# Transpositions of two subchunks at once in the first layer of a four-layer kernel: alternating halves of the array, shared operand tiles

## The chip, the core and the metric

The kernel runs on one core of a Trainium2 chip. Its engines are TensorE (PE in the profile, its weight loads PEld), VectorE (DVE), ScalarE (ACT), GpSimd (POOL) and SyncE (SP), which here only issues DMAs. Matrix products go to PSUM[...]; VectorE and ScalarE carry them from there to SBUF. The metric is the device time of one execution in microseconds (us). All data are 32-bit floats.

## What is computed

Four layers in a row on 8 images of 56 x 56 positions with 192 channels. Only the first is touched. Cut to what matters:

```python
def first_layer(x):                         # x: [8, 56, 56, 192], group-normalised before
    p, q, v = silu(x @ p_w.T + p_b), silu(x @ q_w.T + q_b), silu(x @ v_w.T + v_b)   # 576 channels each
    a1 = rpe_mlp(rpe_input, t1) * decay     # 112 coefficients for each channel
    a2 = rpe_mlp(rpe_input, t2) * decay
    qv = q * v
    o1 = toeplitz(qv along w, a1)           # for each channel a product with a 56 x 56 Toeplitz matrix
    o2 = toeplitz(qv along h, a2)           # the same along the other axis
    return x + (p * (o1 + o2)) @ o_w.T + o_b
```

For each channel d the kernel must form `qv[d] @ A1[d] + A2[d] @ qv[d]` with 56 x 56 matrices. It does both products with one matrix product over 120 partitions: the left operand holds the transposed `qv[d]` in 56 partitions and a Toeplitz matrix in 56 others, the right operand the other two.

## The kernel before, in words

**Tiling.** The 576 channels are 9 subchunks of 64. Two of them make a chunk: chunks 0 to 3 hold subchunks (0,1), (2,3), (4,5), (6,7); chunk 4 is the tail with subchunk 8 alone. In the code `n` counts subchunks through all images, `b` is the image, `c` the chunk.

**What happens to a chunk.**

1. `project` (L283): q and v of the chunk, in four steps `g` of 2 x 7 rows of the image. A step's products (L294 for 128 of the input channels, L301 for the other 64, which lie in two halves of the partitions) go to two PSUM tiles (one in the tail). ScalarE applies SiLU (L310), and `multiply` (L316) writes q*v into the tile `qv` twice, in both orders of rows and columns: "straight" by VectorE (L319), "across" by GpSimd (L325), in the last step partly by VectorE (also L325).
2. `turn` (L342), for one subchunk: 56 transpositions (L352), one for each row position `i`, each of 64 channels by 120 positions out of `qv`, with a piece of the identity matrix. They go into PSUM in steps of up to 16 (16, 16, 16, 8 make 56), eight positions to a bank. After each step VectorE copies partitions 0 to 55 into the left operand and ScalarE partitions 64 to 119 into the right one (both L359). Subchunks with even number lie in partitions 0 to 63 of `qv`, odd ones in 64 to 127; `turn(n)` and then `turn(n + 1)` each stay in one of these halves.
3. `convolve` (L363), for one subchunk: two steps of 32 products (L376) over 120 partitions; results are copied to the tile `ot` (L396 by VectorE, L394 by ScalarE, L387 in the tail).
4. `post` (L407) after chunks 1 and 3, `post_tail` (L495) after the tail: p (`gate`, L417, L424, SiLU L431), transposing `ot` back (`back`, L442) and multiplying (L451 by VectorE), the output product (`out`, L462, L467) and its addition into `acca` and `accb` (L403, L405 by VectorE). `in_turn` orders them: step g is `back(g - 1)`, `gate(g)`, `out(g - 1)`; nine steps in `post`, four in `post_tail`, where the products are L507, L514, L541 and L553, the transpositions L528 and the multiplication L534.

**Operands.** `pairs` (L257) holds two left and two right operand tiles (`ol`, `or`), used by even and odd subchunks. The Toeplitz halves are loaded by `toeplitz(n)` (L265): from the coefficients (`ed`) in the first image, which also writes ready tables (`tt`); from these tables later. `toeplitz(m + 2)` is issued behind `convolve(m)`, on SP's queue.

**PSUM.** One pool of four tiles of two banks each serves the layer, in turn (`banks`, L159): the fifth request waits until the first tile has been read.

**Order.** TensorE's order is that of the program text. `merge(a, b)` (L595) interleaves two lists of steps over as many rounds as the longer has; of the shorter list it places each step at the end of its share of rounds. The loop at L615 does for each chunk: `merge(fill, turns)`, where `fill` is the `post` of the chunks before, if there is one; then `project` of the next chunk, merged with `beside` (statistics and normalisation of images, L98 to L130, L49 and L576); then the convolutions. In chunk 3 `project` of the tail and the convolutions alternate step by step instead (L643). So the transpositions of chunk 0 lie beside the `post_tail` of the image before, those of chunk 2 beside `post(0)`, those of chunk 4 beside `post(1)`; those of chunks 1 and 3 stand alone. The order on the other engines is a scheduler's.

Of the kernel before, what the change touches and what calls it, by code (L numbers as in the profile page):

```python
# [17 lines left out]
H = 56  # L18
# [38 lines left out]
def image_dma(queue, dram, xa, xb, store=False):  # L57


    parts = []  # L60
    for at in range(0, HW, HQ // 2):
        cols = slice(at, at + HQ // 2)
        parts.append((xa[0:CP, cols], dram[:, 0, cols]))
        parts.append((xa[CP:CA, cols], dram[0 : CA - CP, 1, cols]))
        h, own = at // HQ, slice(at % HQ, at % HQ + HQ // 2)
        parts.append((xb[h * CB : (h + 1) * CB, own], dram[CA - CP :, 1, cols]))
    for s, d in parts:
        if store:
            queue.dma_start(d, s)
        else:  # L70
            queue.dma_start(s, d)


def sub(ap, *dims):

    return bass.AP(ap.tensor, ap.offset, [list(ap.ap[0]), *(list(d) for d in dims)])
# [59 lines left out]
def layer0(cx, xin, xout, w, consts):  # L136
# [6 lines left out]
    tc, nc = cx.tc, cx.nc  # L143
    B = len(xin)
    NS, DS = 9, 64
    NC = 5
    NP = 112
    T2, T1 = slice(0, H), slice(64, 64 + H)
    cx.open(B)
    cx.between = ExitStack()  # L150
    with ExitStack() as es:
        gn = GroupNormSplit(cx, cx.between, w["gmat"])
        cp = es.enter_context(tc.tile_pool(name="l0c", bufs=1))
# [5 lines left out]
        def banks():  # L159
            return cx.tile(psc, [128, 2, 512], "c")  # L160
# [4 lines left out]
        def load_raw(b):  # L165
            xa, xb = cx.tile(np_, [CA, HW], "xa"), cx.tile(np_, [128, HQ], "xb")
            image_dma(nc.sync, xin[b], xa, xb)
            return xa, xb
# [3 lines left out]
        ident = cx.tile(cp, [128, 128], "ident")  # L172
# [10 lines left out]
        with ExitStack() as pes:  # L183
# [11 lines left out]
            n = 1  # L195
# [10 lines left out]
            for t in (1, 2):  # L206
# [13 lines left out]
                for i in range(3):  # L220
                    ps = banks()[0:32, 0, 0:NP]
# [3 lines left out]
                e = cx.tile(pp, [DS, NS, NP], f"e{t}")  # L225
                for s in range(NS):
                    ps = banks()[0:DS, 0, 0:NP]
# [23 lines left out]
        qv = cx.tile(cp, [128, H, 120], "qv")  # L251
# [2 lines left out]


        ND = DS * H
        pairs = [tuple(cx.tile(cp, [120, ND + 8], f"o{k}{i}") for k in "lr") for i in range(2)]  # L257
        for pair in pairs:
            for i, t in enumerate(pair):
                (nc.gpsimd, nc.vector)[i].memset(t, 0.0)  # L260

        def channels(t):
            return t[:, 0:ND].rearrange("p (d i) -> p d i", i=H)
# [52 lines left out]
        def multiply(g, rows, ts):  # L316

            def straight():
                nc.vector.tensor_tensor(  # L319
                    sub(qv[rows, 7 * g :, 64 + H - 1 :], (HH * 120, 2), (120, 7), (-1, H)),  # L320
                    *(t.rearrange("p u (h w) -> p u h w", w=H) for t in ts), ALU.mult,
                )

            def across(eng, u, w0, w1):
                eng.tensor_tensor(  # L325
                    sub(qv[rows, w0:, H - 1 - 7 * g - HH * u :], (120, w1 - w0), (-1, 7)),
                    *(t[:, u].rearrange("p (h w) -> p w h", w=H)[:, w0:w1] for t in ts), ALU.mult,
                )

            if g < 3:  # L330
                straight()
                for u in range(2):
                    across(nc.gpsimd, u, 0, H)
                return

            for i, w in enumerate(((0, HH), (HH, H))):
                across(nc.gpsimd, 0, *w)
                across(nc.vector, 1, *w)
                if i == 0:
                    straight()  # L340

        def turn(n):  # L342

            s = n % NS
            e = s % 2 * DS
            left, right = pairs[n % 2]

            def step(i0, ni):
                ps = banks()[0:120]
                view = lambda k: ps[:, k].rearrange("p (d i) -> p d i", i=8)  # L350
                for i in range(ni):
                    nc.tensor.transpose(  # L352
                        view(i // 8)[:, :, i % 8], qv[e : e + DS, i0 + i, :],
                        ident[e : e + DS, e : e + DS],
                    )
                src = ps[:, 0 : ni // 8].rearrange("p k (d i) -> p d k i", i=8)
                for t, rows, copy in ((left, T2, nc.vector.tensor_copy), (right, T1, nc.scalar.copy)):
                    dst = channels(t)[rows, :, i0 : i0 + ni].rearrange("p d (k i) -> p d k i", i=8)
                    copy(dst, src[rows])  # L359

            return [lambda i0=i0: step(i0, min(16, H - i0)) for i0 in range(0, H, 16)]
# [203 lines left out]
        def normalize(xn):  # L565

            measures, deviate, settle = gn.steps(*xn)

            def measure():
                for f in measures:  # L570
                    f()

            def last():
                rstd, nbias = settle(bank)
                affine(nc.vector, xn[0], xn[0], rstd[:, 0:1], nbias[:, 0:1])
                nc.scalar.activation(  # L576
                    xn[1], xn[1], AF.Identity, bias=nbias[:, 1:2], scale=rstd[:, 1:2]
                )

            return [measure, lambda: deviate(bank), last]  # L580

        def tell(b, xa, xb):

            measures, deviate, settle = gn.steps(xa, xb)

            def last(bank):
                nn = cx.tile(gn.small, [128, 2, 2], "nn")
                for i, v in enumerate(settle(bank)):
                    nc.vector.tensor_copy(nn[:, :, i], v)
                nc.sync.dma_start(cx.norms[b][0:CA], nn[:, 0, :])  # L590
                nc.sync.dma_start(cx.norms[b][CA:], nn[0:CB, 1, :])

            return measures, [deviate, last]

        def merge(a, b):  # L595

            n = max(len(a), len(b))
            for i in range(n):
                for x in (a, b):
                    for f in x[i * len(x) // n : (i + 1) * len(x) // n]:  # L600
                        f()

        def new_acc(b):
            acc = cx.tile(xp, [CA, HW], "acca"), cx.tile(xp, [128, HQ], "accb")
            image_dma(nc.sync, xin[b], *acc)
            return acc

        es.enter_context(tc.manual_schedule(engines={mybir.EngineType.PE}))
        xn, nxt = first, None
        merge(normalize(xn), [])  # L610
        for n in range(2):
            toeplitz(n)
        merge(project(xn, 0), [])
        fill, after, telling = [], None, []
        for b in range(B):  # L615
            more = b + 1 < B
            for c in range(NC):
                n = b * NS + 2 * c
                two = c < NC - 1
                turns = turn(n) + (turn(n + 1) if two else [])  # L620
                merge(fill, turns)
                fill, beside = [], []
                if c == 0:
                    if after is not None:
                        image_dma(nc.sync, xout[b - 1], *after, store=True)
                        beside, telling = tell(b - 1, *after)
                    if more:
                        nxt = load_raw(b + 1)
                if c == 1:
                    acc = new_acc(b)  # L630
                    beside = [lambda f=f: f(bank) for f in telling]
                if c == 2 and more:
                    beside = normalize(nxt)

                if c % 2 == 0:
                    ot = cx.tile(cp, [120, 128, H] if two else [H, H, DS], "ot")
                ahead = project(xn, c + 1) if two else project(nxt, 0) if more else []
                convs = []
                for m in (n, n + 1) if two else (n,):
                    *some, last = convolve(m, ot)  # L640
                    convs += some + [lambda m=m, last=last: (last(), toeplitz(m + 2))]

                if c == NC - 2:  # L643
                    ahead = [f for pair in zip(ahead, convs[0:4]) for f in pair]
                    convs = convs[4:]
                merge(ahead, beside)
                for f in convs:
                    f()
                if c in (1, 3):
                    fill = post(c // 2, xn, ot, acc)  # L650
            fill, after = post_tail(xn, ot, acc), acc
            xn = nxt
# [1386 lines left out]
```

## Time and profile before

| | us |
|---|---|
| median of 3 runs | 4290.92 |
| lowest and highest | 4286.24, 4291.43 |
| the profiled execution | 4297.32 |
| its span, from first to last instruction | 4295.5 |

| engine | busy us | share of the span |
|---|---|---|
| PE | 4052.9 | 94% |
| PEld | 2655.7 | 62% |
| DVE | 2340.9 | 54% |
| ACT | 1781.9 | 41% |
| POOL | 1510.6 | 35% |

The profile is one execution. Its groups of instructions are read as: line, engine, operation, output <- inputs, shapes and count, then busy time in us and the mean of one in ns, then the idle time of the engine just before them and what ended it. Matrix products are pipelined: the mean of one is its latency, and busy time over count tells how often one is finished. "The chain" is the work that ended last, followed back from the end; its pieces are start, length, what. Slices of the span are 40 equal parts, with the busy share in tenths. "Stages" are stretches of the span in which busy time of each engine is summed.

### The profile page before, as it was taken

How to read it: one execution, taken by the hardware profiler on the slowest of the kernel's cores; microseconds unless marked ns; L12 is line 12 of the kernel's file. 1: busy time of each engine (PE TensorE's matmuls, PEld its weight loads, DVE VectorE, ACT ScalarE, POOL GpSimd, SP SyncE). 2: the span in 40 equal slices, each digit the busy share in tenths (PEclk: the TensorE clock that was granted, in tenths of full speed). 3: DMA queues.
4: the chain of work that ended last, by engine and by line, in shares of the span. 5: the costliest groups of instructions: out<-in, count | busy, mean ns of one | idle time of the engine just before them, and what ended most of it. 6: DMA issues, size and time to landing. Idle time of an engine off the chain costs nothing.

```text
span 4295.5 us, 106533 instructions
## 1 busy us (share of the span) xinstructions
PE 4052.9 (94%) x46380; PEld 2655.7 (62%) x46380; DVE 2340.9 (54%) x3429; ACT 1781.9 (41%) x2052; POOL 1510.6 (35%) x1295
## 2 busy tenths in 40 slices
PE   6999999999999999999699999769998999998997
PEld 4666767676676767667366666524444555555997
DVE  4446565554656545554444444366665666664664
ACT  2334434334443333443233344223334555554664
POOL 3223232222322222232133333133334444444776
PEclk9999999999999999999899999889999999999999
DMA  6755242242524224241224344455547676664243
GB/s 137 143 106 144 61 114 62 78 96 61 143 62 111 56 74 109 61 109 59 80 72 109 96 107 105 121 173 171 165 140 180 171 174 156 155 152 114 71 117 93
DMA packets 379607, 484.14 MB, mean 113 GB/s; under 512 B 175780, under 2 KB 324372, under 8 KB 377236
## 3 DMA queue, kind: packets, MB, share of 16 engines
q1 hardware_dynamic: 373636, 466.97, 42.8%
q10 hardware_dynamic: 5504, 10.35, 0.8%
q8 instruction: 365, 5.98, 0.6%
q14 instruction: 102, 0.84, 0.1%
HBM read 321.49 MB, written 155.65 MB: 111 GB/s over the span
## 4 chain that ended last, share of the span: by engine, by line
PE 79%; DVE 6%; issue 5%; SPq 3%; DMA 3%; ACT 2%; POOL 1%; DVEq 0%; ACTq 0%; POOLq 0%
PE c L294 10%; PE c L376 6%; PE v L1371 6%; PE c L301 5%; PE c L462 4%; PE c L417 4%; PE c L924 4%; PE h L1873 4%; PE c L352 4%; PE y L959 3%; PE kv L1431 3%; PE c L442 3%; PE c L424 3%; DVE ol L359 2%; PE c L1583 2%
## 5 line engine op out<-in xcount | busy, mean ns | idle before, releaser
L325 POOL TENSOR_TENSOR qv<-s,s 128x392 f32<-128x392 f32 (+3 forms) x320 | 568.5, 1798 | 1453.5 <-ACT s L310 1453.0
L310 ACT ACTIVATE s<-c,bqv 128x784 f32<-128x784 f32 (+1 forms) x320 | 278.2, 910 | 383.9 <-PE c L301 189.1
L294 PE MATMUL c<-xa,wqv 128*128 128x392 f32 x1152 | 433.2, 518 | 4.3 <-DVE xa L49 2.7
L359 ACT COPY or<-c 56x1024 f32<-56x1024 f32 (+1 forms) x288 | 256.2, 901 | 424.4 <-DVE ol L359 414.5
L319 DVE TENSOR_TENSOR qv<-s,s 128x784 f32<-128x784 f32 (+1 forms) x160 | 205.8, 1287 | 265.0 <-ACT s L310 265.0
L359 DVE COPY ol<-c 56x1024 f32<-56x1024 f32 (+1 forms) x288 | 299.8, 1076 | 39.8 <-PE c L352 38.5
L294 PEld LDWEIGHTS c<-xa,wqv 128*128 128x128 f32 x1152 | 211.1, 194 | 176.8 <-issue 39.3
L376 PEld LDWEIGHTS c<-or,ol 120*64 120x64 f32 x9216 | 275.8, 139 | 39.5 <-issue 29.6
L376 PE MATMUL c<-or,ol 120*64 120x56 f32 x9216 | 284.5, 223 | 11.5 <-DMA ol<-ed 7.7
L352 PEld LDWEIGHTS c<-ident,qv 64*120 64x120 f32 x4032 | 256.1, 138 | 55.1 <-issue 35.6
L352 PE MATMUL c<-ident,qv 64*120 64x64 f32 x4032 | 282.8, 224 | 3.6 <-POOL qv L325 2.5
L1371 PE MATMUL v<-wvb,wa 128*128 128x512 f32 (+1 forms) x400 | 192.1, 612 | 50.5 <-ACT wa L1282 31.3
L301 PE MATMUL c<-xb,wqv 64*128 64x392 f32 x1152 | 232.9, 518 | 0.0
L431 ACT ACTIVATE s<-c,bp 128x448 f32<-128x448 f32 x224 | 129.7, 630 | 248.7 <-PE c L424 248.6
L1904 POOL TENSOR_TENSOR y<-y,s 128x448 f32<-128x448 f32 x168 | 185.0, 1101 | 92.7 <-ACT s L1883 92.7
L1873 PE MATMUL h<-ringv,am 128*64 128x57 f32 (+1 forms) x4400 | 192.7, 235 | 19.6 <-DVE ringv L1860 11.8
L462 PE MATMUL c<-po,wo 128*128 128x448 f32 x448 | 198.1, 564 | 7.0 <-DVE po L451 7.0
L1873 PE MATMUL h<-ringh,am 128*64 128x57 f32 (+1 forms) x4400 | 186.3, 232 | 7.8 <-DVE ringh L1879 7.8
L1382 ACT ACTIVATE vb<-sm 128x1024 f32<-128x1024 f32 (+1 forms) x100 | 103.7, 1038 | 212.2 <-issue 187.2
L417 PE MATMUL c<-xa,wp 128*128 128x224 f32 x896 | 191.1, 356 | 0.0
L405 DVE TENSOR_TENSOR acca<-c,acca 128x392 f32<-128x392 f32 (+1 forms) x120 | 67.3, 587 | 219.2 <-PE c L467 204.8
L1873 PEld LDWEIGHTS h<-ringv,am 128*64 128x64 f32 x4400 | 168.1, 140 | 22.9 <-DVE ringv L1860 12.7
(221 smaller groups left out, 7591.9 us busy)
## 6 DMA issues: line engine op xcount, KB each, us to landing
or<-tt SPq DMA_DIRECT2D x252, 196.0 KB
ol<-tt SPq DMA_DIRECT2D x252, 196.0 KB
vt<-v SPq DMA_DIRECT2D x56, 672.0 KB
v<-vb SPq DMA_DIRECT2D x96, 384.0 KB
x<-x SPq DMA_DIRECT2D x112, 168.0 KB
x<-x SPq DMA_DIRECT2D x112, 112.0 KB
bt<-bs SPq DMA_DIRECT2D x28, 448.0 KB
bs<-bs SPq DMA_DIRECT2D x56, 224.0 KB
```

The lines of the kernel that those rows point to most:

```text
L294: nc.tensor.matmul(ps[:, h, 0:n], wqv[0][:, j, :], xn[0][:, at : at + n], start=True, stop=False,)
L301: nc.tensor.matmul(ps[:, h, 0:n], wqv[1][rows, j, :], xn[1][rows, g * n : (g + 1) * n], start=False, stop=True,)
L310: nc.scalar.activation(t, ps[rows, :, 0:n], AF.Silu, bias=bqv[rows, j : j + 1])
L319: nc.vector.tensor_tensor(sub(qv[rows, 7 * g :, 64 + H - 1 :], (HH * 120, 2), (120, 7), (-1, H)), *(t.rearrange("p u (h w) -> p u h w", w= ...
L325: eng.tensor_tensor(sub(qv[rows, w0:, H - 1 - 7 * g - HH * u :], (120, w1 - w0), (-1, 7)), *(t[:, u].rearrange("p (h w) -> p w h", w=H)[:, ...
L352: nc.tensor.transpose(view(i // 8)[:, :, i % 8], qv[e : e + DS, i0 + i, :], ident[e : e + DS, e : e + DS],)
L359: copy(dst, src[rows])
L376: nc.tensor.matmul(ps[u * 64 : (u + 1) * 64, k, v * H : (v + 1) * H], left[:, d * H : d * H + 64], right[:, d * H : (d + 1) * H], start=Tr ...
L417: nc.tensor.matmul(out(u, h), wp[0][:, 2 * j + u, :], xn[0][:, at : at + n], start=(u == 0), stop=True, skip_group_check=True,)
L462: nc.tensor.matmul(pa, wo[:, 2 * j + u, 0:CA], pos[u], start=(u == 0), stop=(u == 1))
L1371: nc.tensor.matmul(out, x[:, at : at + n], wt, start=(k == 0), stop=(k == 1), skip_group_check=True,)
L1873: nc.tensor.matmul(ps[sides[c], y], am[a][:, m * CB : (m + 1) * CB], old[:, x], start=(n < 2), stop=True, skip_group_check=True,)
```

## The change

- The operand tiles become one left and one right tile (`both`), each with the operands of both subchunks: `[120, 2, 64 * 56 + 8]`. `pairs` are views into them.
- A new `turn_both(n)` takes the place of `turn(n) + turn(n + 1)` in chunks 0 to 3. It has seven steps. In each, for eight row positions, one transposition of the subchunk in partitions 0 to 63 and one of that in 64 to 127 follow each other; each subchunk has its own PSUM bank. One copy by VectorE then takes both subchunks' left parts and one by ScalarE both right parts: `56 x 2 x 64 x 8` elements, 1024 in each partition as before, written in runs of 8 where it was 16.
- The tail keeps `turn(n)`.
- `merge` rounds the other way: each step of the shorter list comes at the start of its share of rounds. This holds for all its calls: transpositions beside `post`, `project` beside statistics and normalisation.

```diff
-        pairs = [tuple(cx.tile(cp, [120, ND + 8], f"o{k}{i}") for k in "lr") for i in range(2)]
-        for pair in pairs:
-            for i, t in enumerate(pair):
-                (nc.gpsimd, nc.vector)[i].memset(t, 0.0)
+        both = [cx.tile(cp, [120, 2, ND + 8], f"o{k}") for k in "lr"]
+        for i, t in enumerate(both):
+            (nc.gpsimd, nc.vector)[i].memset(t, 0.0)
+        pairs = [tuple(t[:, k] for t in both) for k in range(2)]
...
+        def turn_both(n):
+
+            order = (n % 2, 1 - n % 2)
+
+            def step(i0):
+                ps = banks()[0:120]
+                view = ps.rearrange("p k (d i) -> p k d i", i=8)
+                for i in range(8):
+                    for e, k in enumerate(order):
+                        rows = slice(e * DS, (e + 1) * DS)
+                        nc.tensor.transpose(
+                            view[:, k, :, i], qv[rows, i0 + i, :], ident[rows, rows]
+                        )
+                for t, rows, copy in zip(both, (T2, T1), (nc.vector.tensor_copy, nc.scalar.copy)):
+                    dst = t[rows, :, 0:ND].rearrange("p k (d i) -> p k d i", i=H)
+                    copy(dst[:, :, :, i0 : i0 + 8], view[rows])
+
+            return [lambda i0=i0: step(i0) for i0 in range(0, H, 8)]
...
             n = max(len(a), len(b))
             for i in range(n):
                 for x in (a, b):
-                    for f in x[i * len(x) // n : (i + 1) * len(x) // n]:
+                    for f in x[-(-i * len(x) // n) : -(-(i + 1) * len(x) // n)]:
                         f()
...
-                turns = turn(n) + (turn(n + 1) if two else [])
+                turns = turn_both(n) if two else turn(n)
```

## The prediction

> **What bounds the kernel now.** I read the two halves of the page first. The first layer is the part of the span before about 2080 us, eight images at about 251 us each.
>
> ```profile
> PE   6999999999999999999699999769998999998997
> PE 79%; DVE 6%; issue 5%; SPq 3%; DMA 3%; ACT 2%; POOL 1%; DVEq 0%; ACTq 0%; POOLq 0%
> ```
>
> TensorE is at 9 in nearly every slice of the first layer, and 79% of the chain is its own work. So time taken from TensorE there shortens the run, unless something else is close behind it. Next, the costliest groups, for the lines that the change touches:
>
> ```profile
> L359 ACT COPY or<-c 56x1024 f32<-56x1024 f32 (+1 forms) x288 | 256.2, 901 | 424.4 <-DVE ol L359 414.5
> L359 DVE COPY ol<-c 56x1024 f32<-56x1024 f32 (+1 forms) x288 | 299.8, 1076 | 39.8 <-PE c L352 38.5
> L352 PE MATMUL c<-ident,qv 64*120 64x64 f32 x4032 | 282.8, 224 | 3.6 <-POOL qv L325 2.5
> ```
>
> 4032 transpositions keep PE busy for 282.8 us, 70 ns each; their copies keep VectorE busy for 299.8 us. The two are equal. ScalarE's copy of a step always starts after VectorE's (414.5 of its 424.4 us idle): a step is evacuated in series, VectorE then ScalarE. Then I cut one image (the third, and chunk 0 of the fourth) into stages:
>
> ```profile
> 661.00:712.00 51.00, 51.00 (x365) 36.33 (x365) 22.40 (x35) 16.77 (x23) 0.00 (x0) 1.00 0.28 56
> 739.00:746.20 7.20, 7.11 (x111) 6.63 (x110) 6.30 (x7) 5.27 (x6) 0.00 (x0) 1.00 0.88 252
> 833.20:853.30 20.10, 20.01 (x207) 12.45 (x205) 17.57 (x24) 10.26 (x11) 0.21 (x1) 0.92 0.66 182
> ```
>
> The columns are length, then PE, weight loads, DVE, ACT and POOL. Beside `post` (661 to 712) VectorE is busy 44%: TensorE alone bounds. With transpositions alone (739 to 746) and beside the tail's `post` (833 to 853) VectorE is at 87%. The chain says what ends the middle one:
>
> ```profile
> 738.78 1.10 PE c L352 x16
> 739.88 0.02 issue
> 739.90 5.22 DVE ol L359 x5
> 745.12 0.02 issue
> 745.14 1.01 ACT or L359
> 746.15 0.04 issue
> 746.20 1.58 PE c L294 x4
> 747.78 0.86 PE c L301 x4
> 748.64 2.01 PE c L376 x64
> ```
>
> One step of 16 transpositions, five copies on VectorE (four of 1.14 us and one half-size of 0.66), one on ScalarE, and only then `project` gets a PSUM buffer. This stage is bound by the evacuation already.
>
> **How fast alternation can be.** The trace of before has no alternating transposition. It has these:
>
> ```profile
> 601.40 2.83 PE c L294 x8
> 604.23 1.52 PE c L301 x8
> ```
>
> ```profile
> 3292.13 0.81 PE c L1569 x56
> ```
>
> L294 has 128 rows; L301 has 64 and goes from half to half: 354 against 190 ns an instruction of 392 columns. L1569 goes round four 64x64 tiles at 14.5 ns an instruction, weight loads of 64 columns included, 58 ns a tile: about what a lone transposition of 64 columns takes (68), so four tiles hide each other wholly.
>
> [...] The new copies write runs of 8 floats[...] where the old wrote 16. No run here shows the new pattern.
>
> **The change part by part.** Call S the time of 16 transpositions. It is 1.09 us now. With full overlap each half does 8 at 68 ns, offset by half a one: 0.58. If instead the weight loads of the two halves are serial, S is worse: L352's loads of 120 columns last 138 ns, like the plain 64-column loads of L467 (136), where plain 128-column ones last 191 (L417); 64 more plain columns cost 55 ns, so I estimate that a transposition's load occupies some 50 ns, and 16 in series 0.8. With no overlap S stays 1.09. I take 0.58: L1569's 58 ns for four 64-column loads excludes serial loading.
>
> A pair of subchunks has 8 steps (six of 16, two of 8: 6 x 1.09 + 2 x 0.61 = 7.76 us of PE) and gets 7 (7S = 4.06). VectorE's copies go from 6 x 1.14 + 2 x 0.66 = 8.16 us to 7 x 1.14 = 7.98: nothing to gain there. By stage and image:
>
> - *Chunk 2, beside `post`.* PE saves 7.76 - 4.06 = 3.70. At the end `back(6)`, one step and `out(6)` follow each other; `out` waits for VectorE's product, which is behind two additions (1.05), the copy before (1.21) and takes 0.63. Before, the 1.09 us step covered this. Counted from the start of the last step but one, the product is there at 3.1 us and PE at 0.58 + 1.08 + 0.58 = 2.24: 0.85 lost. In mid-stage the 2.48 us of `gate` cover the product as before. Gain 2.85.
> - *Chunk 1, alone.* `project` needs the buffer of the fourth copy, now 4 x 1.14 instead of 5.22, and the first copy comes earlier. But VectorE arrives with the backlog of chunk 0 (18 us of copies, additions and statistics that don't shrink, in a stage 1 us shorter), so the first copy starts about 1.0 us into the stage instead of 1.12. 1.0 + 4.56 + 1.02 + 0.04 = 6.62 against 7.43: gain 0.8.
> - *Chunk 3, alone.* Here `convolve` is interleaved with the tail's `project`, and its first step needs subchunk n complete. Before, n was complete after four copies; now both are complete only after seven. S + 0.02 + 7.98 + 1.02 + 0.04 = 9.64 us to the first L376, against 748.64 - 738.78 = 9.86: gain 0.2. The 2.44 us of `project` lie within this wait. This is where the saving of PE is lost.
> - *Chunk 0, beside the tail's `post`.* VectorE's 17.6 us do not shrink. Following the new order by hand (gate, step, back, gate, out, two steps, back, two steps, out, two steps), `project`'s first buffer is freed by the additions of the last `out`, 19.1 us after the convolutions' end; PE's last step ends there too. It is 20.1 now: gain 1.0, give or take 1.
> - *Chunk 4, still one subchunk.* The steps come one place earlier. The stall before the last `out`, 0.95 us (L462 at 808.69, PE free at 807.73), now has no step in front: back(6) at 1.69, product and latency to 2.55, so 0.86. Gain 0.1. The first step, moved ahead, needs GpSimd's first half of L325; that is done about 1 us before PE gets there.
> - *Normalisation one step earlier* (the new rounding in `merge`). ScalarE's table loads (1.28 us each) and the 1.70 us scaling now come before the last SiLU and delay it by about 1.5 us; the convolutions (7.7 us) hide it and leave some 2 us. Nothing, or 1 us an image if that cover fails.
> - *Waits of the shared tile.* The table loads of SP still wait for the convolution of their own subchunk, and are issued in the same order. No new wait.
>
> Sum: 2.85 + 0.8 + 0.2 + 1.0 + 0.1 = 4.95 us an image; seven images 35. The first has no tail beside chunk 0, and its chunk 3 waits for a table load anyway (14.65 us of DMA in the chain at 235.61); I count 5 for it. Together 40 us: the profiled execution, 4295.5 of span and 4297.3 in all, would become 4257; the median of the runs shown, 4290.9, which is 6.4 below it, 4251.
>
> **The rivals.** A measurement of this kernel can tell about 0.2% (9 us) from no change.
>
> - *Loads partly serial* (S = 0.8): chunk 2 gains 7.76 - 5.60 - 0.63 = 1.5, the others 0.65, 0, 0.85, 0.1: 3.1 an image, 25 us, 4266. For it: L424 alternates too and takes 120 ns where L417 takes 190, less than half off. Against: L1569.
> - *No overlap at all* (S = 1.09), the change not doing what it says: chunk 2 loses 0.2, chunk 3 0.3, the others gain 0.9 together: 0.4 an image, 4288, no change. Against it stands L301.
> - *Slower: the copies' short runs.* If runs of 8 cost VectorE more, all seven copies of chunks 0 and 3 and four of chunk 1 lengthen the path, 18 an image, plus one in chunk 2. L325 on VectorE, with runs of 7 and strided reads, takes 540 ns for 196 elements where a copy of 2 elements (L121) takes 159: 1.9 ns an element against 1.0. At that price a copy costs 0.9 us more: 17 us an image lost, 12 net, 8 x 12 = 97, 4388. It decides from 0.26 us a copy (4.95 / 19). [...]
>
> **How the numbers follow.** Full overlap 0.58, own range 4238 to 4263 (chunk 0's give or take 1 and the first image's 5). Partly serial 0.17. No overlap 0.10. Slower copies, or another wait of that size, 0.11. A gain above 55 us 0.04. Faster by over 0.2%: 0.58 + 0.17 + 0.04 less the edge of the second, 0.78. Within 0.2%: 0.11. Slower: 0.11. The range leaves out the slow rival and the large gain: 4236 to 4290.
>
> **What would show it.** Right: L352 near 36 ns of PE busy each for the paired ones; ol copies still near 1.14 us each in a row; in chunk 3 a wait of L376 for ScalarE's last copy; VectorE's share in the chain up; an image 5 us shorter. Wrong: L352 still at 65 to 70 ns; a copy over 1.3 us; a DMA ahead of L376 in images after the first; GpSimd ahead of L352.

## The result, and the profile after

| | before | after |
|---|---|---|
| median | 4291.18 us (4 runs) | 4258.02 us (4 runs) |
| lowest and highest | 4286.24, 4297.21 | 4253.59, 4265.11 |
| span of the profiled execution | 4295.5 | 4263.3 |

The ratio is 0.9924, with an interval of 0.9905 to 0.9942: 33 us faster. The forecast was 4251, with a range of 4236 to 4290. Of the four executions after, the profiled one was the slowest (4265.11).

The page of the kernel after, first the chain of waits by engine, then the groups of the touched lines, in the columns named above (L352 keeps its number, VectorE's and ScalarE's copies are now L357, the convolution is L395):

```profile
PE 73%; DVE 7%; issue 7%; DMA 4%; SPq 3%; POOL 3%; ACT 2%; DVEq 0%; POOLq 0%; ACTq 0%
...
L357 DVE COPY ol<-c 56x1024 f32<-56x1024 f32 x224 | 261.4, 1208 | 63.4 <-PE c L352 63.4
...
L352 PE MATMUL c<-ident,qv 64*120 64x64 f32 x3584 | 144.3, 227 | 44.2 <-ACT or L357 38.3
```

A transposition in pairs occupies PE for 144.3 / 3584 = 40 ns, where it was 70. The copies are as long as before: 1208 ns for 1024 elements. New is the last column of L352: PE now stands before its transpositions for 44.2 us, nearly all of it until ScalarE's copy. TensorE's share of the chain fell from 79% to 73%. TensorE now waits more for the engines that empty PSUM.

A table by stage shows where the 33 us came from. It is worked out from the start times of TensorE's instructions in the traces; means over images 1 to 7 (counted from 0, so that the third image is image 2), in us. A stage runs from the start of the last convolution before it to the first product of what follows, and the convolutions of chunk 1 from their first to their last product:

| stage | before | after | late_norm | old_rounding | no_alternation | steps_only | fill_chunk1 |
|---|---|---|---|---|---|---|---|
| chunk 0, beside the tail's `post` | 20.07 | 19.80 | 19.43 | 20.67 | 20.14 | 21.01 | 19.42 |
| chunk 1, alone, then `project` of chunk 2 | 27.89 | 26.21 | 26.49 | 26.16 | 26.68 | 26.56 | 24.90 |
| convolutions of chunk 1 | 7.49 | 8.54 | 7.47 | 7.55 | 8.69 | 7.51 | 7.47 |
| chunk 2, beside `post(0)` | 51.27 | 49.21 | 48.24 | 48.39 | 50.34 | 49.86 | 48.24 |
| chunk 3, to its first convolution | 10.02 | 10.11 | 10.13 | 10.22 | 10.80 | 10.31 | 10.23 |
| chunk 4, beside `post(1)` | 48.31 | 48.15 | 48.15 | 48.30 | 48.15 | 48.31 | 48.15 |
| start of the layer's last 128 convolution products, at | 2075.8 | 2045.6 | 2028.7 | 2036.8 | 2066.2 | 2057.4 | 2017.5 |

The last five columns are experiments 1, 4, 3, 4 and 6 below. The last row stands for the end of the layer; what follows it, with the last `post_tail` and the three untouched layers, took 2207 to 2220 us in these seven. Each column is one execution, and the profiled one is not always a middling one: 7 us above the median in the kernel after, 6 us below it in late_norm, 15 us below it in old_rounding. So a difference between last rows carries these offsets, and a stage is the safer evidence where its seven images agree.

**Chunk 2, beside `post`.** The end of this stage in the third image, in the chain of the kernel after (start, length, what):

```profile
693.00 0.61 PE c L352 x16
693.62 1.10 PE c L461 x8
...
695.14 0.61 DVE po L470
695.75 0.04 issue
695.80 1.77 PE c L481 x4
```

A step of 16 takes 0.61 us. Behind `back(6)` (L461) TensorE waits 1.08 us for VectorE's product (L470), which stands behind a copy. Five of seven images take 48.24 to 48.32 here, 3.0 less than before; image 6 took 54.32, see the first experiment.

**Chunk 3.** The same view, fourth image:

```profile
975.04 0.64 PE c L352 x16
...
975.70 8.02 DVE ol L357 x7
...
983.74 1.01 ACT or L357
...
984.79 2.15 PE c L395 x64
```

Seven copies of VectorE in a row, 1.14 us each, one of ScalarE, and then the convolution: 975.04 to 984.79 is 9.75 us. What TensorE saved lies within these 8 us.

**Chunk 1.** The same view, third image:

```profile
618.79 1.01 ACT or L357
619.80 0.04 issue
619.85 1.11 PE c L352 x16
620.96 0.02 issue
620.98 3.92 PE c L294 x8
```

A step of 0.61 us takes 1.11 and L294 takes 3.92 in place of 2.83. The windows of the two stretches (length, busy PE, weight loads, DVE, ACT, POOL, then the granted clock, the DMA engines' busy share and GB/s) say why:

```profile
613.00:619.80 6.80, 5.02 (x152) 4.54 (x148) 5.44 (x5) 3.93 (x4) 0.00 (x0) 0.99 0.86 213
619.80:625.20 5.40, 5.33 (x26) 3.15 (x28) 3.48 (x4) 4.03 (x4) 0.00 (x0) 0.70 0.96 231
```

The granted clock averages 0.70 behind a stretch in which TensorE was busy for 5.02 of 6.80 us.

**The convolutions of chunk 1** are the only stage that got clearly longer. Chain of the kernel after, fourth image:

```profile
890.57 7.60 PE c L395 x254
898.17 1.67 issue
899.84 0.32 PE c L395 x2
```

TensorE stops for 1.67 us, two records from the end of a step of 64, with no engine named. Five other images have stops of 0.3 to 0.9 us elsewhere, within a step too (after 153 records in the third); image 6 has none here. A wait for a PSUM tile would stand at the start of a step. The page has a queue of the kind "instruction":

```profile
q8 instruction: 365, 5.98, 0.6%
```

These are 365 blocks of 16 KB. The queue is taken for TensorE's: in the packet records of both traces, of before and after, one block starts for each 256.0 of TensorE's instructions (2 x 46380 = 92760 in the page, 93467 and 93474 with those of its sequencers), and none lies more than 0.93 of a block off that line. Counted by the instructions of VectorE, ScalarE, GpSimd or SyncE, some lie 18 to 35 blocks off. Beside the stop the packet records have a block that arrives at 898.29 (897.40 and 0.89 us under way), and TensorE goes on at 899.84, 1.55 us later. In this layer TensorE takes instructions fastest in a convolution stage, 512 in 7.5 us. What is different in this stage is what `merge` puts beside the `project` ahead of it. In chunk 1 that is the end of the statistics of the image before: a square root and the stores of two norms, called the normalisation below, as in the prediction. Timelines of the kernel after and of the kernel before, same image (start, length, engine, line):

```profile
886.50 1.28 ACT L128 ACT_TABLE_LOAD   x1
...
890.61 0.35 SPq L609 DMA_DIRECT2D norm<-nn  x1
...
891.29 1.72 ACT L310 ACTIVATE s<-c,bqv 128x784 f32<-128x784 f32 x2
```

```profile
905.26 1.72 ACT L310 ACTIVATE s<-c,bqv 128x784 f32<-128x784 f32 x2 [2.63 <-POOL qv L325]
...
906.73 7.55 PEld L376 LDWEIGHTS c<-or,ol 120*64 120x64 f32 x256
906.99 1.28 ACT L128 ACT_TABLE_LOAD   x1
...
911.77 0.35 SPq L590 DMA_DIRECT2D norm<-nn  x1
```

Before, the last SiLU began 1.5 us ahead of the convolutions and the stores of the norms 5.0 us behind their start. After, the square root and its table come first, the SiLU begins 0.8 us behind the start, and the stores come 0.1 us behind it.

### The profile page after: what moved, and what is told of

It is laid out like the page before. It is cut to its first block, busy times and chain, and to the rows that moved or that the text cites. A ratio compares the mean times of both kernels' runs of the same rounds, so it can differ in the third digit from the quotient of the medians.

```text
span 4263.3 us, 106441 instructions
## 1 busy us (share of the span) xinstructions
PE 3954.9 (93%) x46380; PEld 2553.1 (60%) x46380; DVE 2345.1 (55%) x3396; ACT 1781.1 (42%) x2020; POOL 1512.6 (35%) x1294
## 4 chain that ended last, share of the span: by engine, by line
PE 73%; DVE 7%; issue 7%; DMA 4%; SPq 3%; POOL 3%; ACT 2%; DVEq 0%; POOLq 0%; ACTq 0%
PE c L294 9%; PE v L1390 6%; PE c L395 6%; PE h L1892 5%; PE c L301 5%; PE c L481 4%; PE c L436 4%; PE c L943 4%; PE c L461 3%; PE y L978 3%; PE kv L1450 3%; PE c L443 3%; PE c L486 2%; DVE ol L357 2%; PE c L949 2%
## 5 line engine op out<-in xcount | busy, mean ns | idle before, releaser
L325 POOL TENSOR_TENSOR qv<-s,s 128x392 f32<-128x392 f32 (+3 forms) x320 | 569.3, 1799 | 1424.6 <-ACT s L310 1354.2
L294 PE MATMUL c<-xa,wqv 128*128 128x392 f32 x1152 | 435.9, 520 | 7.7 <-ACT or L357 4.8
L319 DVE TENSOR_TENSOR qv<-s,s 128x784 f32<-128x784 f32 (+1 forms) x160 | 190.4, 1190 | 268.2 <-ACT s L310 268.1
L357 ACT COPY or<-c 56x1024 f32<-56x1024 f32 x224 | 225.6, 1007 | 256.3 <-DVE ol L357 240.9
L294 PEld LDWEIGHTS c<-xa,wqv 128*128 128x128 f32 x1152 | 212.2, 196 | 177.2 <-issue 44.2
L395 PEld LDWEIGHTS c<-or,ol 120*64 120x64 f32 x9216 | 277.8, 138 | 55.7 <-issue 47.4
L395 PE MATMUL c<-or,ol 120*64 120x56 f32 x9216 | 287.2, 223 | 18.5 <-DMA ol<-ed 9.0
L357 DVE COPY ol<-c 56x1024 f32<-56x1024 f32 x224 | 261.4, 1208 | 63.4 <-PE c L352 63.4
L481 PE MATMUL c<-po,wo 128*128 128x448 f32 x448 | 198.1, 564 | 10.8 <-DVE po L470 10.8
L436 PE MATMUL c<-xa,wp 128*128 128x224 f32 x896 | 192.0, 358 | 3.2 <-issue 3.2
L352 PE MATMUL c<-ident,qv 64*120 64x64 f32 x3584 | 144.3, 227 | 44.2 <-ACT or L357 38.3
L943 PE MATMUL c<-wv,xc 128*126 128x192 f32 x896 | 175.4, 339 | 0.7 <-DVE s L903 0.6
```

The lines of the kernel that those rows point to most:

```text
L294: nc.tensor.matmul(ps[:, h, 0:n], wqv[0][:, j, :], xn[0][:, at : at + n], start=True, stop=False,)
L319: nc.vector.tensor_tensor(sub(qv[rows, 7 * g :, 64 + H - 1 :], (HH * 120, 2), (120, 7), (-1, H)), *(t.rearrange("p u (h w) -> p u h w", w= ...
L325: eng.tensor_tensor(sub(qv[rows, w0:, H - 1 - 7 * g - HH * u :], (120, w1 - w0), (-1, 7)), *(t[:, u].rearrange("p (h w) -> p w h", w=H)[:, ...
L357: copy(dst[:, :, :, i0 : i0 + 8], view[rows])
L395: nc.tensor.matmul(ps[u * 64 : (u + 1) * 64, k, v * H : (v + 1) * H], left[:, d * H : d * H + 64], right[:, d * H : (d + 1) * H], start=Tr ...
L436: nc.tensor.matmul(out(u, h), wp[0][:, 2 * j + u, :], xn[0][:, at : at + n], start=(u == 0), stop=True, skip_group_check=True,)
```

## The experiments

All ratios are against the kernel before, run on the same chip. The edits are shortened to the lines that matter.

**1. Normalisation back in its place.**

```diff
-                merge(ahead, beside)
+                merge(ahead, beside, True)    # True: round as the kernel before
```

> The changed kernel, but `merge(ahead, beside)` rounds as before, so that statistics and normalisation stand where they stood; transpositions keep the new rounding. Theory 1 (the cover of the normalisation fails: the square root's table load comes before the last SiLU of `project`, so the last multiplications and then the copies to `ot` are late): the convolutions of chunk 1 are back at 7.46 us from first to last product (8.5 in the mean in the changed kernel) and the late `post` of image 6 (54.3 us where the others have 48.3) goes too: 8 x 1.0 + up to 6 us less, 4244 to 4250. Rival (the stretched convolutions come from the turns in both halves, by the clock or by the copies): no difference, 4258.

4246.16 us, ratio 0.9905 (0.9884 to 0.9925), as theory 1 expected. The convolutions of chunk 1 take 7.47 us again, 7 x 1.07 = 7.5 us less, and no image has a late `post`. That the earlier normalisation lengthens these convolutions is shown, here and in experiment 2. By the ratios, 0.9905 against 0.9924, it costs some 8 us in all, though the two intervals overlap. The layer ends 16.9 us earlier than in the kernel after, which says too much: the profiled execution of the kernel after was the slowest of four, that of this kernel the fastest of five. Of the difference 6.8 us lie in chunk 2, nearly all in image 6 alone, 2.6 in chunk 0, whose order this edit leaves as it is, and 3.8 in the first image, of which 2.4 were there at the end of the convolutions of its chunk 1, before the edit changes anything.

The reason that theory 1 gives, the copies to `ot`, is not the right one: but for one, TensorE's stops are not at the start of a step. Their times go with the blocks of instructions instead. In the four kernels that have the normalisation early (after, and before_early, no_alternation and old_turns_chunk3 of experiments 2, 3 and 5) TensorE stopped 33 times for over 0.3 us in convolutions behind the first image, 7 to 11 us in each kernel; 24 of the stops ended 0.9 to 1.9 us after a block of instructions had arrived, 22 of these 1.2 to 1.6 us after it, seven more ended while one was under way, and two have no block near. Before, late_norm, old_rounding, steps_only and fill_chunk1 have five such stops together, 2.7 us. In image 6 of the kernel after a stop of 3.10 us ahead of the first `gate` is of the same kind (block there at 1646.62, L436 at 1648.08), and most of the rest of its 6 us is a lower clock behind it (granted clock 0.50 from 1647.07 to 1653.90): L436 x8 took 3.36 us, where it takes 1.71. No experiment changed the instruction stream by itself: that the stops are waits for instructions is an inference from the times and not shown.

If they are, why the blocks come late is open. Some blocks were long under way behind the stores (3.49 us from 393.25, stores' packets from 391.56), others started late. Slow blocks behind the stores are not new: in the kernel before one took 2.79 us from 408.14, 1.51 us behind the first store, but the convolutions were over 0.9 us after it had started, and no stop followed in them. So the stores' new place, early in the convolutions, is a likely part of it, by the author's estimate from these times. The amount of traffic does not explain it: in the kernel after the convolutions of chunk 2 have more (DMA share 0.46 against 0.36) and no stop. A kernel with the arithmetic early and only the stores late was not tried.

**2. The rounding alone, in the kernel before.**

```diff
-                    for f in x[i * len(x) // n : (i + 1) * len(x) // n]:
+                    for f in x[-(-i * len(x) // n) : -(-(i + 1) * len(x) // n)]:
```

> The kernel before, with only the new rounding in `merge`. Theory 1: the normalisation one step earlier costs the convolutions of chunk 1 about 1 us an image here as well (7.46 becomes about 8.5), and the last `out` of each `post` loses the small step that covered its wait, 0.3 to 0.8 us: 8 to 20 us slower, 4299 to 4311. Rival (rounding costs nothing): 4291.

4301.4 us, ratio 1.0022 (1.0015 to 1.0030): 9 us slower, as theory 1 expected. The convolutions of chunk 1 take 8.98 us in the mean (7.49 before), so this loss does not come from the turns in both halves; `post(0)` is 0.07 us longer in the median, not 0.3 to 0.8. The profiled execution was the fastest of its kind (4290.67) and is of no use for a sum: in it `project` of chunk 2 never met the lower clock, 1.06 us an image less than before.

**3. No alternation.**

```diff
-                for i in range(8):
-                    for e, k in enumerate(order):
+                for e, k in enumerate(order):
+                    for i in range(8):
```

> The changed kernel, but each step transposes eight positions of one subchunk and then eight of the other, so that consecutive transpositions stay in one half; tiles, banks, copies and order of steps as changed. Theory (the gain is the overlap of halves): a step takes 1.09 us again where it takes 0.62; beside `post` 7 x 0.47 = 3.3 us lost, of which the stall at the last `out` gives back some 0.5; chunk 3 loses 0.5, chunks 0 and 1 up to 1 together: about 4 us an image, 32 us, 4290. Rival (the gain comes from seven steps of full size in place of eight, and from the order): at most 5 us lost, 4258 to 4263.

4280.21 us, ratio 0.9969 (0.9961 to 0.9977): 19 us of the 33 are lost by the ratios, 22 by the medians, between the two expectations. The chain of this kernel at the end of chunk 2 shows which number was wrong:

```profile
698.60 0.91 PE c L352 x16
699.51 1.08 PE c L461 x8
700.59 0.90 PE c L352 x16
701.50 1.70 PE c L481 x4
```

A step takes 0.91 us, not 1.09, and no wait is left before `out` (L481). The median of this stage is 49.72 against 48.25: 7 x (0.91 - 0.62) = 2.0, less part of the 1.08 us that the longer step covers. The starts of the single transpositions explain the 0.91. In the kernel before they follow each other at 59 ns, and the first gap of a step is 107. In the kernel after two start within some 4 ns of each other, and such pairs follow at 59 ns. Without alternation they follow at 59 ns, but around the one change of half inside a step three start within 2 to 7 ns of their neighbour. TensorE overlaps the halves there too, over a few instructions.

**4. The old rounding, with and without alternation.** Every `merge` rounds as in experiment 2's removed line. The first kernel has both halves, common tiles and copies, and nothing else of the change; the second takes alternation away from it as in experiment 3.

> The changed kernel with the old rounding in every `merge`, so that only the transpositions in both halves, the shared operand tiles and the common copies are left of the change. Theory 1 (all that the new rounding costs is the late SiLU): as the run with only the normalisation moved back, 4246 within 4. Rival (the new rounding of the turns beside `post` also has a price or a gain): its difference from 4246 is that price; more than 6 us either way would show it.

> The changed kernel with the old rounding everywhere and without alternation: what is left of the change is seven full steps for a pair of subchunks in place of eight (six full, two half), in common tiles, with one change of half in each step. Theory (three parts that add up: alternation 22 us, as measured with the new rounding; this rest; the rounding, a gain of the turns and a loss of the normalisation that nearly cancel): 1.4 us less beside `post` and 0.7 less in chunk 1 than before, nothing in chunk 3: 2.1 x 8 = 17 us under the kernel before, ratio 0.996, 4279 on these chips. Rival (without alternation nothing is left of the gain): 4296, ratio 1.000.

4260.74 us, ratio 0.9927 (0.9909 to 0.9944), and 4271.0 us, ratio 0.9953 (0.9939 to 0.9967). By the ends of the layer the parts are: seven full steps in common tiles 2075.8 - 2057.4 = 18 us, of which 10.7 lie in the first image; alternation 2057.4 - 2036.8 = 21 us, the same as in experiment 3 (2066.2 - 2045.6 = 21); the new rounding of the turns 2036.8 - 2028.7 = 8 us, in chunk 0 (20.67 against 19.43, 7 x 1.24 = 8.7). The new rounding of the normalisation goes the other way, by some 8 us as in experiment 1. The medians of these two kernels lie only 10 us apart, and the profiled execution of the first is the fastest of its six. The interval of each is some 7 us to either side. So the size of alternation is not settled here: 10 to 21 us. The expectation of 4246 for the first missed by more than its 6 us: the rounding of the turns is a gain, which the rival had named. The second came 8 us below its 4279, and its rival of 4296 is out.

**5. Old turns in chunk 3.**

```diff
-                turns = turn_both(n) if two else turn(n)
+                if two and c < NC - 2:
+                    turns = turn_both(n)
+                else:
+                    turns = turn(n) + (turn(n + 1) if two else [])
```

> The changed kernel, but chunk 3 uses the old `turn(n)` and `turn(n + 1)` one after the other; chunks 0 to 2 alternate. Theory (in chunk 3 the saving of TensorE lies inside the wait for the copies, since both subchunks are now complete only together): from the last convolution of chunk 2 to the first of chunk 3 it takes 10.0 us either way; no difference, 4258 within 3. Rival (alternation saves TensorE's time there too): 7.76 - 4.3 = 3.4 us an image lost, 4285.

4262.61 us, ratio 0.9934 (0.9917 to 0.9950), which the after's 0.9924 can't be told from. To the first convolution it takes 10.02 us in this kernel and 9.98 (median) in the kernel after. The rival of 4285 is out: in chunk 3 alternation brings nothing.

**6. Work in TensorE's wait of chunk 1.** On top of experiment 1, `project` of chunk 2 gives its first step in two halves, and the first of them stands behind the fourth step of the transpositions:

```diff
+                if c == 1:
+                    ahead = project(xn, 2, split=True)     # q's product, v's product, steps 1 to 3
+                    turns = turns[:4] + [ahead[0]] + turns[4:]
                 merge(fill, turns)
```

> The changed kernel with the old rounding for the normalisation, and in chunk 1 the first step of `project` split into its two products (q, then v), with q's placed behind the fourth step of the transpositions and v's behind the seventh, so that TensorE has work in the wait for the copies. Theory (this stage is bound by seven copies on VectorE, TensorE stands idle in it[...]): from the last convolution of chunk 1 to the second step of `project` 9.6 to 10 us in place of 11.0, and no product of L294 at half rate behind it (1.0 to 1.7 us in some images): 1.2 us an image for the order and up to 0.8 for the clock, 8 to 16 us less than 4246: 4230 to 4238. Rival (the products only push the last transpositions and copies back): 4246.

4235.0 us, ratio 0.9867 (0.9851 to 0.9882), as the theory expected and below the kernel after (0.9924) as well as the kernel before. Chunk 1 with the next `project` takes 24.90 us, 1.6 less than in experiment 1, and 24.82 in six of seven images. In those six no product ran at a lower clock, where two images of experiment 1 lost 1.69 us to it and one 1.0. So the order alone is worth 25.86 - 24.82 = 1.0 us an image, and the rest is the clock.

**7. The same in chunk 3.**

> As the kernel that fills chunk 1, and in chunk 3 the first step of the tail's `project` stands behind the fourth step of the transpositions too. Theory (TensorE's saving in chunk 3 lies in the wait of the first convolution): the 2.4 us of that step go into the wait, and the copies come some 0.7 us later: 1.7 us an image, 13 us less than the kernel that fills chunk 1 alone, 4217 to 4225. Rival (the convolution is moved back by as much as is taken out of its path): no difference from that kernel.

4279.62 us, ratio 0.9977 (0.9967 to 0.9986). This kernel put the whole step ahead, with its multiplication into `qv`. The last three steps of the transpositions then read the tail's products in a part of subchunk 6, and had to wait for GpSimd (3.88 us at L347). To the first convolution it took 19.6 us. It says nothing on the theory. The next kernel has the first step's multiplication as a step of its own, behind the seventh:

```diff
+                if c == 3:
+                    ahead = project(xn, 4, split=True)     # product and SiLU; multiplication; steps 1 to 3
+                    turns = turns[:4] + [ahead[0]] + turns[4:]
...
-                    ahead = [f for pair in zip(ahead, convs[0:4]) for f in pair]
+                    rest, *ahead = ahead[1:]
+                    ahead = [rest] + [f for pair in zip(ahead, convs[0:3]) for f in pair] + convs[3:4]
```

> As the kernel that fills chunks 1 and 3, with one mistake of order mended: there the multiplication of the tail's first step stood ahead of the last three steps of the transpositions, so that these waited for GpSimd (and read the tail's products); now only its matrix product and SiLU stand behind the fourth step, the multiplication behind the seventh. Theory (in chunk 3 TensorE's saving lies in the wait of the first convolution): 1.7 us an image less than with chunk 1 filled alone, 13 us: 4222 within 6. Rival (the copies are moved back by as much as the path is relieved): 4235.

4239.27 us, ratio 0.9865 (0.9850 to 0.9880): no different from the kernel that fills chunk 1 alone. The rival holds, and the chain of this kernel in chunk 3 shows where:

```profile
719.45 1.28 ACT L332
...
722.60 2.84 ACT or L384 x3
...
725.48 2.15 PE c L422 x64
```

The SiLU of the step moved ahead, with its table load (L332), stands for 3.1 us on ScalarE in front of the last three copies. TensorE's 2.4 us went into the wait, and the wait grew by the same amount (12.59 us to the first convolution, where it was 10.0, with 2.5 us less behind it).

**8. Two steps of `project` ahead of the first convolution of chunk 3**, with the transpositions left alone, on top of experiment 6:

```diff
-                    ahead = [f for pair in zip(ahead, convs[0:4]) for f in pair]
+                    first, *ahead = ahead
+                    ahead = [first] + [f for pair in zip(ahead, convs[0:3]) for f in pair] + convs[3:4]
```

> As the kernel with chunk 1 filled; in chunk 3 the transpositions are left alone, but two steps of the tail's `project` stand ahead of the first convolution in place of one, and the other steps follow each by each. Theory (TensorE waits about 1 us between the first step of `project` and the first convolution, and a second step that needs no copy fills this wait): the first convolution starts 1.4 us later but has 2.4 us less behind it: up to 1 us an image, 8 us less than 4235, 4227. Rival (the SiLU of these steps pushes ScalarE's last copies back, as where a step stood among the transpositions): 4235 or more.

4233.34 us, ratio 0.9858 (0.9843 to 0.9872): the lowest of all, but not to be told from 0.9867, and between the two expectations. By the profile the layer ends at 2011.5, 6 us before that of experiment 6. In five of seven images L294 of the first step lost about 1 us of the gain to a lower clock (2.60 us in place of 1.51 at 719.26, at a granted clock of 0.69 from 719.20 to 722.70).

**9. VectorE relieved in chunk 0.** On top of experiment 1, ScalarE takes the left copies of two of seven steps:

```diff
-                for t, rows, copy in zip(both, (T2, T1), (nc.vector.tensor_copy, nc.scalar.copy)):
+                left = nc.scalar.copy if i0 in given else nc.vector.tensor_copy   # given: (16, 40) in chunk 0
+                for t, rows, copy in zip(both, (T2, T1), (left, nc.scalar.copy)):
```

> The changed kernel with the old rounding for the normalisation, and in chunk 0 ScalarE takes the left copies of the third and the sixth step of the transpositions too, 2 x 1.14 us that VectorE no longer does. Theory (beside the tail's `post` VectorE bounds, so alternation gained little there): the stage of 19.4 us loses 1 to 2.3 us, 8 to 18 us in all: 4228 to 4238. Rival (TensorE or ScalarE bounds this stage): 4246.

4248.48 us, ratio 0.9891 (0.9874 to 0.9907): no gain; the stage took 19.49 us against 19.43. In experiment 1 VectorE made a copy of 1.21 us just ahead of the product that `out` waits for. Here the chain has two pieces of statistics in that place (L115, 1.08 us at 826.95). The scheduler filled the freed time with other work: in the stage, means of seven images, VectorE's copies fell from 5.90 to 4.76 us, the statistics rose from 1.09 to 2.26, and VectorE was busy for 16.38 us where it was 16.33. So this kernel did not take load off VectorE in the stage. Whether the load as a sum or what stands in front of the product sets the stage stays open. An order with nothing in front of it was not tried.

**10. Chunks 1 and 3 filled and VectorE relieved.**

> Both of these together: chunks 1 and 3 filled, VectorE relieved in chunk 0. If the stages add up: the two gains together, 4204 to 4216. If one of them only shifts a wait into the other's stage: no better than the better of the two.

4236.99 us, ratio 0.9864 (0.9850 to 0.9879): no better than experiment 6, as its second case says.

## Why the prediction was right, and where it was off

- *S = 0.58.* Measured 0.61 to 0.64: full overlap, by experiment 3 and by the starts in pairs. The "partly serial" rival (0.8) is out.
- *Chunk 2, 2.85.* Measured 3.0. The wait for the product that was to appear (0.85) did, at 1.08.
- *Chunk 1 alone, 0.8.* From the last convolution to L294 it took 7.65 us and takes 6.64: 1.0. The mechanism is as predicted, L294 behind ScalarE's fourth copy, with one thing added: in the third image the seventh step of transpositions, at the lower clock, covers most of that wait.
- *Chunk 3, 0.2.* The first convolution was put at 9.64 us and came at 9.75 in the fourth image, behind ScalarE's last copy; the stage as a whole gained nothing. That TensorE's saving is lost there is shown by experiment 5.
- *Chunk 0, 1.0 give or take 1.* Measured 0.27, within the bound; 0.64 with the normalisation back in its place. Its reason was that VectorE's 17.6 us do not shrink. They shrank in the stage, from 17.55 to 16.70 (means of seven images), and experiment 9, which was to test the reason, left VectorE's load where it was; the reason is open.
- *Chunk 4, 0.1.* Measured 0.16.
- *Normalisation, "nothing, or 1 us an image if that cover fails".* This is the term that was mis-sized: the sum took nothing. It measured 1.05 us an image in the convolutions, some 8 us in all by the ratios of experiment 1 and 9 by experiment 2. The SiLU came 2.3 us later, where 1.5 was predicted, and the convolutions did cover that; what they did not cover, and what the working never looked at, is stops of TensorE, nearly all within its steps and with no engine named (7 to 11 us in each of the four kernels of experiment 1 that have the normalisation early).
- *The shared tile.* No wait for a DMA of the table loads in chunks 1 to 4 of later images, as said.
- *The first image, 5.* By the layer's progress at its `post(1)` it was 7.4, in one execution.

The change is all in the layer. In the two profiled executions the 40 us became 30.2 there (2075.8 to 2045.6), and 33 us in the medians. With the normalisation put back the gain is 41 us by the ratio of experiment 1 (0.9905 of 4291), and the seven images gain 5.1 us each by the table, where 4.95 was forecast. So the forecast of 40 us holds but for the one term that was set to nothing. Its parts are less exact than its sum: chunk 1 with the `project` behind it gained 1.4 for 0.8, chunk 0 0.64 for 1.0, chunk 3 nothing for 0.2, and that these cancel is luck. The first image came 11.2 us earlier in experiment 1, where 5 was counted, but in it single executions differ by 2.4 us where the kernels do not, as told there. The lower clock was not counted at all: `project` of chunk 2 lost 1.69 us to it in four of seven images before, 1.0 and 1.7 in two of them after.

Slower copies: the rival is out. Seven runs-of-8 copies in a row took 8.02 us, as much per copy as the runs of 16. Its price was also read from one of two kinds: of the L325 instructions of 196 elements on VectorE one takes 0.54 us (at 830.53 in the kernel before) and the next 1.25 (at 832.59); the prediction used the first alone. "The two are equal", of 282.8 and 299.8 us, is loose too; nothing rests on it.

## What to carry to other kernels

Where an engine becomes faster, look stage by stage at who empties its buffers: here 3.0 of the 3.7 us that TensorE saves counted beside `post`, and none in chunk 3, where seven copies stood in series. Work put into a wait pays only if what follows from it (here a table load and two SiLU, 3.1 us) does not stand in front of the copies that end the wait. And when steps shift by one place, a stretch with many short instructions may be no free cover for small DMAs (here 512 took 8.54 us, and 7.47 with statistics and normalisation back in their place): read the packets of the instruction queue beside the stops that no engine explains.

## What the runs showed of the hardware

TensorE stops where no engine holds it, shown as "issue" in the middle of a step or ahead of one, 0.3 to 3.1 us a time, and goes on mostly 1.2 to 1.6 us after a block of the instruction queue has arrived (22 of 33 stops in convolutions), as told above. What it waits for is not shown.

In the traces of the kernels before and after, the records of the granted clock (44 and 52) know 1.00 and 0.50 alone, and its changes lie multiples of 3.41 us apart. Means such as 0.70 are mixtures. In chunk 1 of the kernel after the clock fell behind gaps of at most 0.93 us, and in the kernel before, in every second image, behind a stretch with hardly a gap (windows of the fourth image; its L294 x8 then took 4.59 us):

```profile
878.30:885.70 7.40, 7.37 (x114) 6.89 (x112) 6.24 (x6) 5.41 (x6) 0.00 (x0) 1.00 0.91 227
885.70:890.40 4.70, 4.63 (x10) 2.33 (x11) 1.83 (x3) 2.51 (x4) 0.00 (x0) 0.64 1.00 211
```

The first row holds the 112 transpositions of the chunk, each in one half of the array, and next to nothing else, and PE counts as busy for 7.37 of 7.40 us. The clock is 1.00 from 882.50 to 885.91, with PE busy for 3.31 us, and 0.50 from 885.91 to 889.32. So the busy share of a profile does not show what the clock goes by, and what it does go by is not shown by any run here. At the same order of work it fell in some images and not in others (at `project` of chunk 2 in the kernel before in four of seven).

Transpositions of the two halves overlap not only in pairs: in experiment 3 one change of half in 16 was enough for 1.09 us to become 0.91.
